# Perceiver megakernel on one core: three of thirteen subtractions of the maximum on GpSimd, full turns of the last context rows, scan rows fetched singly

## The chip, the cores and the metric

The kernel runs as one program on one core of a Trainium2 chip. The core has TensorE (PE; its weight loads are listed apart as PEld), VectorE (DVE), ScalarE (ACT), GpSimd (POOL) and SyncE (SP), which here only issues DMAs. The metric is the device time of one execution in microseconds (us); the median of three runs is shown, and a few tenths of a per cent is what two runs differ by.

## The reference

Two layers work on a latent array x of 16 batches x 64 rows x 128 columns, with a context of 16 x 1601 x 128. Each layer is cross-attention, then a state-space block, then a feed-forward block, each added to x. Cut to what matters here:

```python
# cross-attention, 16 heads of 64, softmax over 1601 context rows and 64 latents
logits = einsum('bhld,bhsd->bhls', q * scale, k * scale)   # layer 1 masks some rows
w = softmax(logits, axis=-1)
out = einsum('bhls,bhsd->bhld', w, v).reshape(B, L, INNER) @ Wo
# state-space block of layer 0, a scan over 64 positions for each of 16 states
h = dA * h + dB * z_t[:, :, None]
y_t = einsum('bds,bs->bd', h, C_t)
```

## The kernel before

**Groups and steps.** The attention is worked in 64 groups: 2 layers x 16 batches x 2 halves of the heads. A group has 512 queries (8 heads x 64 latents) and 13 tiles of 128 context rows, twelve of the context (G = 12) and one of 64 context rows (REM) and the 64 latents; the one context row that is left over is handled apart (`apart`, `apart_weight`). The projections of keys and values are folded into the queries and the output weights, so a tile's scores are one matmul of the turned context `kvT` against the queries. One step n of the main loop in `run` (L1584) is one tile: `scores` (L693) multiplies into a PSUM bank `s` (three such banks), DVE takes the running maximum `R` over the tiles (L714 in layer 1, with the mask; L716 in layer 0), and ACT copies the scores to SBUF as `st` (L719 or L721). 23 steps (LAG) later `average` (L810) multiplies the weights with the context rows `kv` into `av`.

**The maximum.** When a group's 13 tiles are scored, `plan` (L1533) runs it through stages, counted in steps after its end. Step 0, `partial`: a reduction of R on DVE over blocks (L750) and `four` (L751). Step 2, `joint`: a transpose on PE (L758) and a reduction on DVE, `top` (L760). Step 3, `handed`: two DMAs, one on ACT's queue back into R (L765), one on SP into DRAM, `md` (L766). Step 5, `everywhere`: DVE spreads R's rows into `mb`, one of the three PSUM banks of the pool `tp` (L772). Step 7, `own_max`: SP reads md back as a column (L779). Step 11: the weight of the row apart (L786, L787). The last group has a plan of its own (`maximum`, `spread_max`).

**The weights.** From step 6 on, every second step, `weigh` (L802) takes two tiles: DVE subtracts mb from them in place (L807), ACT takes the exponential (L808). The seven calls have 2, 2, 2, 2, 2, 2 and 1 tiles, at steps 6 to 18; the last two are tiles 10 and 11, and tile 12. mb is released after the last of them. `gather` (L822) then forms the averages `aq` on DVE, `denominator` (L865) divides them on POOL (L869), `turn` (L871) transposes them and `output` (L886) multiplies with the output weights.

**Context.** `context` (L628) normalises a batch's context in layer 0, writes it to DRAM (`xh`), turns it on PE in four calls of up to four blocks (L685; the last call is one block of 64 rows), and ACT scales each call twice, into `kvT` and into `kts`, which goes to DRAM for layer 1. The rows 64 to 127 of the last block are set to zero beforehand (L518, L656). `with_latents` (L612) multiplies kv by the norm's weights on POOL (L624).

**Scan.** `scan0` (L899) works on 256 of 1024 rows at a time. For each of 16 states s, `ahead` (L969) makes the decays `da` on ACT (L977) and the inputs `db` on POOL (L978); then come DVE's scan (L989), DVE's product with the row of C (L994) and POOL's sum (L995). The rows of B and C for a state are broadcast from DRAM to all partitions as `bb` (L974), for two states at a time, in two DMAs, with two buffers.

**What sets the order.** The text of the program gives each instruction its priority; a scheduler at build time then fixes each engine's order, an instruction going as soon as its inputs are expected to be there. `behind` (L1662) keeps side work behind the last score work on PE, ACT and DVE. On the chip every engine and every DMA queue works in that fixed order. Side work (context, queries, scan, experts, feed-forward) is drawn in between by budgets in `run`.

**cT.** In `scan1` (L1223) a tile `cT` holds the rows of C for layer 1's block (L1326); `th` (L1252) is the tile of a tanh that is read last at L1282.

Of the kernel before, what the change touches and what calls it, by code (L numbers as in the profile page):

```python
# [32 lines left out]
F32 = mybir.dt.float32  # L33
# [4 lines left out]
ALU = mybir.AluOpType  # L38
# [4 lines left out]
P = 128  # L43
NB, L, D = 16, 64, 128
# [3 lines left out]
G = 12  # L48
REM = 64
# [4 lines left out]
NQ = 512  # L54
# [2 lines left out]
PAIRS = 13  # L57
BLK = 32
LOWEST = -3.0e38

(LN1W, LN1B, LN2W, LN2B, NORMW, NORMB, G1, G2, YG1, YB1, YG2, YB2) = range(12)
LNOFF = 12
# [5 lines left out]
NS = 16  # L68
# [10 lines left out]
TG = CG * P  # L79
# [4 lines left out]
class Kernel:  # L84
# [543 lines left out]
    def context(self, lay, b):  # L628

        nc = self.nc  # L630
        w1, b1 = self.vecs_of(lay)[:2]
        kv, kvT = self.kv_of[lay, b]
        n = G + 1
        if (lay, b) == (0, 1):

            mv = self.sm([P, n, 2], "fmv", bufs=2)
            rstd, off = (self.sm([P, n], f"c{x}") for x in ("rstd", "off"))
            for k in range(n):
                bs = self.sm([P, 6], "fbs")
                nc.vector.bn_stats(bs, kv[:, k, :D])  # L640
                nc.vector.bn_aggr(mv[:, k, :], bs)
                if k % 2:
                    yield 1.0
            nc.vector.tensor_scalar_add(rstd, mv[:, :, 1], EPS)
            self.rsqrt(rstd, rstd, n)
            nc.gpsimd.tensor_tensor(off, mv[:, :, 0], rstd, ALU.mult)
            nc.gpsimd.tensor_scalar(off, off, -1.0, None, ALU.mult)
            for k in range(8, n):
                nc.gpsimd.tensor_scalar(kv[:, k, :D], kv[:, k, :D], mv[:, k, 0:1], rstd[:, k:k + 1], ALU.subtract, ALU.mult)
            yield HOP3  # L650
            for k in range(8):
                nc.scalar.activation(kv[:, k, :D], kv[:, k, :D], AF.Identity, scale=rstd[:, k:k + 1], bias=off[:, k:k + 1])
                if k % 2:
                    yield 1.0
        elif lay == 0:
            nc.gpsimd.memset(kv[64:P, G, :D], 0.0)  # L656
            nmean, rstd, v, off = (self.sm([P, n], f"c{x}") for x in ("mean", "rstd", "var", "off"))
            for lo, hi in ((0, 7), (7, n)):
                nc.vector.tensor_reduce(nmean[:, lo:hi], kv[:, lo:hi, :D], AX.X, ALU.add)
                if lo == 0:  # L660
                    yield 1.0
            nc.vector.tensor_scalar_mul(nmean, nmean, -1.0 / D)
            yield 0.2
            for k in range(n):
                scr = self.at.tile([P, D], F32, tag="cscr", name=f"scr{b}_{k}", bufs=1)
                nc.scalar.activation(scr, kv[:, k, :D], AF.Square, bias=nmean[:, k:k + 1], accum_out=v[:, k:k + 1])  # L666
                if k in (3, 6, 9):
                    yield 0.0
            yield HOP1
            nc.vector.tensor_scalar(v, v, 1.0 / D, 1e-5, ALU.mult, ALU.add)  # L670
            self.rsqrt(rstd, v, n)
            nc.gpsimd.tensor_tensor(off, nmean, rstd, ALU.mult)  # L672
            yield HOP5
            for k in range(n):
                nc.scalar.activation(kv[:, k, :D], kv[:, k, :D], AF.Identity, scale=rstd[:, k:k + 1], bias=off[:, k:k + 1])  # L675
                if k in (3, 6, 9):
                    yield 0.0
        if lay == 0:
            nc.sync.dma_start(out=self.xh[b], in_=kv[:, :, :D])
            yield HOP  # L680
            for g in range(G // 4 + 1):
                w, m = (512, P) if g < G // 4 else (REM, REM)
                t = self.tp(f"kt{b}_{g}")
                for k in range(4 * g, min(4 * g + 4, n)):
                    nc.tensor.transpose(t[:, (k - 4 * g) * P:(k - 4 * g) * P + m], kv[:m, k, :D], self.ident[:m, :m])  # L685
                raw = self.at.tile([P, 512], F32, tag="kts", name=f"kts{b}_{g}", bufs=1)
                for to, by in ((kvT[:, g * 512:g * 512 + w], w1), (raw[:, :w], YG1)):
                    nc.scalar.activation(to, t[:, :w], AF.Copy, scale=self.vcol[:, by:by + 1])
                nc.sync.dma_start(out=self.xhT[b][:, g * 512:g * 512 + w], in_=raw[:, :w])
                yield HOP3  # L690
        yield from self.with_latents(lay, b)
# [76 lines left out]
    def everywhere(self, g):  # L768
# [2 lines left out]
        grp["mb"] = self.tp(f"mb{g}")  # L771
        self.nc.vector.stream_shuffle(grp["mb"], grp["R"], [0] * BLK)  # L772

    def own_max(self, g):

        nc, grp = self.nc, self.groups[g]
        m4 = grp["m4"] = self.sm([P, 4], "m4")
        with nc.allow_non_contiguous_dma(reason="one number for each query"):
            nc.sync.dma_start(out=m4, in_=self.mdram[g].rearrange("(k f) j -> (f j) k", k=4))  # L779
# [22 lines left out]
    def weigh(self, g, j):  # L802

        nc, grp = self.nc, self.groups[g]
        st, mb = grp["st"][j], grp["mb"]
        n = min(2, NT - 2 * j)
        nc.vector.tensor_tensor(st, st, self.row(mb, [P, n, NQ]), ALU.subtract)  # L807
        nc.scalar.activation(st, st, AF.Exp)  # L808

    def average(self, g, i, j):  # L810
# [88 lines left out]
    def scan0(self, gr):  # L899
        nc, tc, a = self.nc, self.tc, self.a  # L900
        X = self.X[:, gr * CG:(gr + 1) * CG, :]
        with tc.tile_pool(name="sc1", bufs=1) as one, ExitStack() as later:
            t1 = lambda shape, name: one.tile(shape, F32, tag=name, name=f"sc_{name}")
# [21 lines left out]
            both = [P, 2, TG]  # L925
# [7 lines left out]
            g = self.tp("g")  # L933
            for k in range(2):
                nc.tensor.matmul(g[:, k * TG:(k + 1) * TG], W_gate[:, k * P:(k + 1) * P], xT, start=True, stop=True)
            th = t1(both, "y")
# [11 lines left out]
            t = self.tp("bc")  # L948
# [3 lines left out]
            bcd = self.dram.tile([2, NS, TG], F32, tag=f"bcd{gr}", name=f"bcd{gr}")  # L952
# [13 lines left out]
            y = t1(both, "y")  # L966
            yield 1.2

            def ahead(s):  # L969
                nonlocal bb  # L970
                if s % 2 == 0:
                    bb = work.tile([P, 2, 2, TG], F32, tag="bb", name=f"bb{s}")
                    for j in range(2):
                        nc.sync.dma_start(out=bb[:, j], in_=bcd[j, s:s + 2, :].partition_broadcast(P))  # L974
                da, db = (work.tile(both, F32, tag=n, name=f"{n}{s}") for n in ("da", "db"))
                for k in range(2):
                    nc.scalar.activation(da[:, k, :], dt[:, k, :], AF.Exp, scale=na[:, k, s:s + 1])  # L977
                nc.gpsimd.tensor_tensor(db, u, self.row(bb[:, 0, s % 2, :], both), ALU.mult)  # L978
                return da, db, self.row(bb[:, 1, s % 2, :], both)

            bb = None
            made = ahead(0)
            yield HOP
            for s in range(NS):
# [238 lines left out]
    def scan1(self, c0, CG):  # L1223
# [5 lines left out]
        with tc.tile_pool(name="sd1", bufs=1) as one, tc.tile_pool(name="sd2", bufs=CG) as work:  # L1229
# [93 lines left out]
                        nc.tensor.matmul(t[:, hh * TG:(hh + 1) * TG], m[:, k, hh * P:(hh + 1) * P], xc[:, k, :], start=(k == 0), stop=(k == 1))  # L1323
                nc.scalar.copy(dst.rearrange("p h t -> p (h t)"), t[:, :2 * TG])

            bT, cT = t1([P, 2, TG], "bT"), t1([P, 2, TG], "cT")  # L1326
            bc(bT, BwT)
            yield 0.4
            yield HOP1
# [198 lines left out]
    def run(self, out):  # L1528
# [2 lines left out]
        self.groups = [{"key": (lay, b, half)} for lay in range(2) for b in range(NB) for half in range(2)]  # L1531
        ng = len(self.groups)
        self.plan = (  # L1533
            ((0, self.partial), (2, self.joint), (3, self.handed), (5, self.everywhere), (7, self.own_max), (11, self.apart_weight)),
            ((1, self.maximum), (3, self.spread_max)),
        )
        per_layer = NB * 2 * NT
# [251 lines left out]
```

## Time and profile before

| | us |
|---|---|
| median of three runs | 1936.54 (1932.92 to 1939.88) |
| the profiled execution | 1938.11 |
| its span, first to last instruction | 1936.4 |
| PE busy | 1883.0 |
| PEld busy | 1426.3 |
| DVE busy | 1633.4 |
| ACT busy | 1357.9 |
| POOL busy | 511.8 |
| the subtractions L807 on DVE, 448 | 461.3 (two tiles each) + 42.9 (one tile) |
| the exponentials L808 on ACT, two tiles each, 384 | 404.1 |
| mean granted TensorE clock | 0.996 of full |

All lines of the profile name a line of the kernel, an engine, an operation and the tile that is written, an arrow, and the tiles that are read, with buffer numbers left out. "busy" is the time in which the engine works on at least one instruction of the group; "idle before" is the time in which it stood still ahead of them, and what ended that. In the list of waits, "ACT st L719 <- DVE R L714" says that ACT stood still ahead of its instruction on st at L719 until DVE's instruction on R at L714 had ended. "issue" is time with no wait that the profile shows.

### The profile page before, as it was taken

Reading aid. Unit: us, or ns where it says so; the run is one execution under the profiler, and the core shown is the slowest. Engines: PE = TensorE matmul, PEld = TensorE weight load, DVE = VectorE, ACT = ScalarE, POOL = GpSimd, SP = SyncE. Lnnn points to the kernel's source line nnn. Section 1 sums busy time; section 2 is a strip of 40 time slices with the busy share of each in tenths; the row PEclk is TensorE's granted clock in tenths of the full one; section 3 lists DMA queues with packets and bytes.
Section 4 is the critical chain, followed back from the end, with each engine's and each line's share of the span. In section 5 each row is a group of like instructions: output and inputs, shape, how many; then the busy total and the mean of one; then the engine's idle time right before and its main releaser. Section 6 shows DMA issues by size and latency. Waiting matters only on the chain. (4 is left out here: it accounts for less than half of the span.)

```text
span 1936.4 us, 32717 instructions
## 1 busy us (share of the span) xinstructions
PE 1883.0 (97%) x11738; PEld 1426.3 (74%) x11738; DVE 1633.4 (84%) x3186; ACT 1357.9 (70%) x2635; POOL 511.8 (26%) x584
## 2 busy tenths in 40 slices
PE   9999999998999999999999999999999999999998
PEld 5777777676777767777667787767778777776786
DVE  7987777998878998886998978999787998877984
ACT  5888887897869888776665757767566565765651
POOL 5122122543214453121443203453101121102000
PEclk9999999999999999999999999999999999999999
DMA  6121112321123131232232102222120211201100
GB/s 194 36 58 55 55 55 77 86 64 45 54 82 94 57 82 49 69 95 68 73 79 59 40 25 75 71 71 55 42 58 21 60 38 38 59 2 38 25 2 23
DMA packets 192268, 112.64 MB, mean 58 GB/s; under 512 B 56030, under 2 KB 174570, under 8 KB 192106
## 3 DMA queue, kind: packets, MB, share of 16 engines
q1 hardware_dynamic: 187278, 109.77, 20.6%
q8 instruction: 93, 1.52, 0.3%
q10 hardware_dynamic: 4828, 0.78, 0.2%
q14 instruction: 69, 0.57, 0.1%
HBM read 81.41 MB, written 27.54 MB: 56 GB/s over the span
## 5 line engine op out<-in xcount | busy, mean ns | idle before, releaser
L820 PEld LDWEIGHTS av<-kv,st 128*128 128x128 f32 x6656 | 870.2, 192 | 365.6 <-issue 346.3
L820 PE MATMUL av<-kv,st 128*128 128x129 f32 x6656 | 884.6, 276 | 2.2 <-DVE aq L829 2.1
L706 PE MATMUL s<-qT,kvT 128*128 128x512 f32 x1664 | 862.8, 601 | 15.7 <-ACT st L721 10.5
L808 ACT ACTIVATE st<-st 128x1024 f32<-128x1024 f32 (+1 forms) x448 | 444.4, 997 | 130.2 <-DVE st L807 124.2
L807 DVE TENSOR_TENSOR st<-st,mb 128x1024 f32<-128x1024 f32 (+1 forms) x448 | 504.2, 1130 | 2.0 <-PE mb L794 1.5
L719 ACT ACTIVATE st<-s,mcol 128x512 f32<-128x512 f32 x416 | 282.7, 683 | 219.4 <-DVE R L714 197.5
L721 ACT COPY st<-s 128x512 f32<-128x512 f32 x416 | 239.9, 582 | 108.1 <-DVE R L716 100.2
L714 DVE SCALAR_TENSOR_TENSOR R<-s,mcol,R 128x512 f32<-128x512 f32 x352 | 261.5, 743 | 57.2 <-PE s L706 55.2
L716 DVE TENSOR_TENSOR R<-s,R 128x512 f32<-128x512 f32 x352 | 240.2, 682 | 67.0 <-PE s L706 65.2
L706 PEld LDWEIGHTS s<-qT,kvT 128*128 128x128 f32 x1664 | 254.8, 192 | 35.9 <-ACT st L721 18.4
L624 POOL TENSOR_TENSOR kv<-kv,vec 128x384 f32<-128x384 f32 (+1 forms) x128 | 133.7, 1059 | 242.6 <-PE kt L685 68.9
L869 POOL TENSOR_TENSOR aq<-aq,rd 128x512 f32<-128x512 f32 x63 | 71.7, 1138 | 254.4 <-DVE rd L868 241.7
L978 POOL TENSOR_TENSOR db<-sc_u,bb 128x512 f32<-128x512 f32 x64 | 84.9, 1329 | 120.1 <-DVE h L989 61.2
L995 POOL TENSOR_TENSOR sc_y<-sc_y,h 128x512 f32<-128x512 f32 x60 | 79.6, 1327 | 117.6 <-DVE h L994 116.9
L989 DVE TENSOR_TENSOR_SCAN h<-da,db 128x512 f32<-128x512 f32 x64 | 85.7, 1339 | 0.0
L675 ACT ACTIVATE kv<-kv,coff,crstd 128x128 f32<-128x128 f32 x182 | 77.9, 494 | 8.5 <-POOL coff L672 8.5
L829 DVE SCALAR_TENSOR_TENSOR aq<-xeb,ee,av 128x129 f32<-128x129 f32 x252 | 76.7, 339 | 0.6 <-issue 0.4
L666 ACT ACTIVATE scr<-kv,cmean 128x128 f32<-128x128 f32 x182 | 72.3, 397 | 0.8
L498 PE MATMUL q<-xnT,wqk 128*128 128x128 f32 x512 | 68.4, 277 | 2.7 <-ACT qT L507 2.3
L498 PEld LDWEIGHTS q<-xnT,wqk 128*128 128x128 f32 x512 | 63.0, 192 | 7.7 <-ACT qT L507 2.5
L139 POOL TENSOR_TENSOR crstd<-cvar,neghalf 128x13 f32<-128x13 f32 x14 | 34.8, 2487 | 120.5 <-DVE cvar L670 98.9
L892 PEld LDWEIGHTS o<-wvo,aT 128*128 128x128 f32 x512 | 59.4, 192 | 5.3 <-issue 3.6
(425 smaller groups left out, 1821.4 us busy)
## 6 DMA issues: line engine op xcount, KB each, us to landing
bb<-bcd SPq DMA_DIRECT2D x64, 256.0 KB
xh<-kv SPq DMA_DIRECT2D x16, 832.0 KB
kv<-xh SPq DMA_DIRECT2D x16, 832.0 KB
kvT<-xhT SPq DMA_DIRECT2D x16, 800.0 KB
kv<-in_ctx_dram SPq DMA_DIRECT2D x15, 768.0 KB
xhT<-kts SPq DMA_DIRECT2D x45, 256.0 KB
ew<-in_e1T_dram SPq DMA_DIRECT2D x36, 64.0 KB
ew<-in_e3T_dram SPq DMA_DIRECT2D x36, 64.0 KB
```

Source lines behind the costliest of these rows:

```text
L498: nc.tensor.matmul(t[:, k * P:(k + 1) * P], self.wqk[:, g * 4 + k, :], xnT, start=True, stop=True)
L624: nc.gpsimd.tensor_tensor(kv[:, lo:hi, :D], kv[:, lo:hi, :D], self.row(self.vec[:, w1, :], [P, hi - lo, D]), ALU.mult)
L706: mm = nc.tensor.matmul(s, self.kv_of[lay, b][1][:, i * P:(i + 1) * P], q, start=True, stop=True)
L714: mx = nc.vector.scalar_tensor_tensor(R, s, mc, last, ALU.add, ALU.max)
L716: mx = nc.vector.tensor_tensor(R, s, last, ALU.max)
L719: ev = nc.scalar.activation(st, s, AF.Identity, bias=mc)
L721: ev = nc.scalar.copy(st, s)
L807: nc.vector.tensor_tensor(st, st, self.row(mb, [P, n, NQ]), ALU.subtract)
L808: nc.scalar.activation(st, st, AF.Exp)
L820: nc.tensor.matmul(grp["av", j][:, k, :], st, self.kv_of[lay, b][0][:, i, :], start=(i == 0 and k == 0), stop=(i == NT - 1 and k == 1))
L978: nc.gpsimd.tensor_tensor(db, u, self.row(bb[:, 0, s % 2, :], both), ALU.mult)
L989: nc.vector.tensor_tensor_scan(flat(h), flat(da), flat(db), 0.0, ALU.mult, ALU.add)
```

## The change

For all groups but the last, weigh steps 5 and 6 no longer subtract on DVE. A new stage at step 6 broadcasts md from DRAM to all partitions (`wide`, one buffer of 128 x 512 in SBUF), and three new stages at steps 10, 12 and 14 subtract wide from tiles 10, 11 and 12 on POOL, in place. In `context` the last block is turned with all 128 rows; only its first 64 columns are used, as before. In `scan0` the rows of one state come in one DMA, for the current and the next state, in three buffers of half the size. In `scan1` cT takes the buffer of th. Each of these two gives back 2 KB of every partition in its own stage; wide takes 2 KB in all of them.

```diff
+SIDE = (10, 11, 12)
...
             for g in range(G // 4 + 1):
-                w, m = (512, P) if g < G // 4 else (REM, REM)
+                w = 512 if g < G // 4 else REM
                 t = self.tp(f"kt{b}_{g}")
                 for k in range(4 * g, min(4 * g + 4, n)):
-                    nc.tensor.transpose(t[:, (k - 4 * g) * P:(k - 4 * g) * P + m], kv[:m, k, :D], self.ident[:m, :m])
+                    nc.tensor.transpose(t[:, (k - 4 * g) * P:(k - 4 * g + 1) * P], kv[:, k, :D], self.ident)
...
+    def broadcast(self, g):
+        wide = self.groups[g]["wide"] = self.at.tile([P, NQ], F32, tag="wide", name=f"wide{g}", bufs=1)
+        self.nc.sync.dma_start(out=wide, in_=self.mdram[g].rearrange("c j -> (c j)").partition_broadcast(P))
+    def lowered(self, g, i):
+        grp = self.groups[g]
+        st = grp["st"][i // 2][:, i % 2, :]
+        self.nc.gpsimd.tensor_tensor(st, st, grp["wide"], ALU.subtract)
...
-        nc.vector.tensor_tensor(st, st, self.row(mb, [P, n, NQ]), ALU.subtract)
+        if g == len(self.groups) - 1 or 2 * j not in SIDE:
+            nc.vector.tensor_tensor(st, st, self.row(mb, [P, n, NQ]), ALU.subtract)
         nc.scalar.activation(st, st, AF.Exp)
...
+            def fetch(s):
+                x = fetched[s] = work.tile([P, 2, TG], F32, tag="bb", name=f"bb{s}", bufs=3)
+                nc.sync.dma_start(out=x, in_=bcd[:, s, :].partition_broadcast(P))
             def ahead(s):
-                nonlocal bb
-                if s % 2 == 0:
-                    bb = work.tile([P, 2, 2, TG], F32, tag="bb", name=f"bb{s}")
-                    for j in range(2):
-                        nc.sync.dma_start(out=bb[:, j], in_=bcd[j, s:s + 2, :].partition_broadcast(P))
+                for x in range(s, min(s + 2, NS)):
+                    if x not in fetched and x not in done:
+                        fetch(x)
+                bb = fetched.pop(s)
+                done.add(s)
...
-                nc.gpsimd.tensor_tensor(db, u, self.row(bb[:, 0, s % 2, :], both), ALU.mult)
-                return da, db, self.row(bb[:, 1, s % 2, :], both)
+                nc.gpsimd.tensor_tensor(db, u, self.row(bb[:, 0], both), ALU.mult)
+                return da, db, self.row(bb[:, 1], both)
...
-            bT, cT = t1([P, 2, TG], "bT"), t1([P, 2, TG], "cT")
+            bT, cT = t1([P, 2, TG], "bT"), one.tile([P, 2, TG], F32, tag="th", name="sd_cT")
...
-            ((0, self.partial), (2, self.joint), (3, self.handed), (5, self.everywhere), (7, self.own_max), (11, self.apart_weight)),
+            ((0, self.partial), (2, self.joint), (3, self.handed), (5, self.everywhere), (6, self.broadcast), (7, self.own_max), (11, self.apart_weight),
+             *((10 + 2 * k, lambda p, i=i: self.lowered(p, i)) for k, i in enumerate(SIDE))),
```

More of the change, by code (lines that the diff above doesn't have):

```diff
@@ L977, in ahead @@
                     nc.scalar.activation(da[:, k, :], dt[:, k, :], AF.Exp, scale=na[:, k, s:s + 1])
-                nc.gpsimd.tensor_tensor(db, u, self.row(bb[:, 0, s % 2, :], both), ALU.mult)
-                return da, db, self.row(bb[:, 1, s % 2, :], both)
-            bb = None
+                nc.gpsimd.tensor_tensor(db, u, self.row(bb[:, 0], both), ALU.mult)
+                return da, db, self.row(bb[:, 1], both)
+            fetched, done = {}, set()
             made = ahead(0)
```

## The prediction

> **What bounds the kernel now.** I read the page's first part, then the busy times by stretch, then the waits of PE, ACT and DVE, and last the groups by shape.
>
> ```profile
> PE 1883.0 (97%) x11738; PEld 1426.3 (74%) x11738; DVE 1633.4 (84%) x3186; ACT 1357.9 (70%) x2635; POOL 511.8 (26%) x584
> ```
>
> PE is the bound: 53.4 us of 1936.4 idle. No change off PE can give more than that, and much of it lies where this change doesn't act. Busy times by stretch (us of PE, PEld, DVE, ACT, POOL; instructions in brackets):
>
> ```profile
> 100.00:1800.00 1700.00, 1660.71 (x10280) 1256.44 (x10279) 1452.10 (x2733) 1226.50 (x2371) 466.97 (x503) 1.00 0.21 58
> ...
> 300.00:400.00 100.00, 95.58 (x548) 69.24 (x547) 88.42 (x144) 82.45 (x175) 44.33 (x40) 1.00 0.31 85
> ...
> 500.00:600.00 100.00, 100.00 (x605) 77.87 (x605) 81.33 (x186) 76.92 (x181) 20.79 (x28) 1.00 0.19 52
> ...
> 700.00:800.00 100.00, 93.84 (x603) 69.95 (x602) 84.23 (x141) 82.18 (x187) 31.93 (x31) 1.00 0.22 61
> ...
> 1400.00:1500.00 100.00, 100.00 (x680) 78.97 (x679) 80.21 (x169) 59.96 (x100) 11.72 (x17) 0.99 0.15 40
> ```
>
> Between 100 and 1800 us PE idles 1700 - 1660.7 = 39.3 us; the other 14 are the start and the tail, which the change leaves alone. Sort the 17 stretches of 100 us by DVE's share: in the eight with DVE at 83.5 us or less PE idles 7.1 us in all (0.9 each), in the nine above it 32.2 (3.6 each). So PE starves where DVE is full. The waits say how (total us, times, longest):
>
> ```profile
> ACT st L719 <- DVE R L714: 197.5, 202, 5.5
> ACT st L808 <- DVE st L807: 124.2, 186, 3.3
> ACT st L721 <- DVE R L716: 100.2, 104, 4.3
> ...
> PE s L706 <- ACT st L721: 10.5, 15, 1.7
> PE s L706 <- ACT st L719: 4.6, 8, 1.1
> PE tm L758 <- DVE four L751: 3.6, 6, 1.3
> ```
>
> The running maximum R, in DVE's queue behind the subtractions, holds ACT's copy of the scores; that copy frees the PSUM bank, and the next score matmul waits for it. Of PE's idle time 24.1 us is named after DVE's or ACT's lateness in this loop: 15.1 (scores), 3.6 (tm), 2.2 (WvT for X, L896), 2.1 (av for aq, L829), 1.1 (mq for L807).
>
> **The subtractions leave DVE.** Groups by shape (busy, mean ns, idle before):
>
> ```profile
> L807 DVE TENSOR_TENSOR st<-st,mb 128x1024 f32<-128x1024 f32 x384 | 461.3, 1207 | 2.0 <-PE mb L794 1.5
> ...
> L989 DVE TENSOR_TENSOR_SCAN h<-da,db 128x512 f32<-128x512 f32 x64 | 85.7, 1339 | 0.0
> ...
> L994 DVE TENSOR_TENSOR h<-h,bb 128x512 f32<-128x512 f32 x60 | 48.0, 799 | 0.0
> ...
> L807 DVE TENSOR_TENSOR st<-st,mb 128x512 f32<-128x512 f32 x64 | 42.9, 671 | 0.0
> ```
>
> There are 2 layers x 16 batches x 2 halves = 64 groups; all but the last lose weigh step 5 (tiles 10 and 11) and step 6 (tile 12): 63 x (1207 + 671 ns) = 118.3 us off DVE. They run back to back (idle before 2.0 us), so they are queue that R, top and aq stand behind, not path by themselves: what they are worth is what PE waits for that queue.
>
> **They arrive on POOL.** 63 x 3 = 189 subtractions of 128x512 with both inputs in SBUF. L978 and L995 are the same shape: median 1273 ns each (the means, 1329 and 1327, include collisions). 189 x 1.27 = 240 us; POOL goes from 512 to 752 us, 39%. POOL isn't on PE's path while it is on time. Is it? In the timeline of each of the 63 groups, counted from the end of top (L760): the m read (L779), which waits for the landing of md just as the new broadcast will, issues after 1.4 us (median; at most 7.0). A 256 KB bb transfer took 3.4 to 4.4 us from issue to the start of the waiting db. So wide is there after some 5.3 us (at most 11.4), and three subtractions end 3.8 us later: 9.1, at most 15.2. The exponential of tiles 10 and 11 starts now after 26.0 us (median), 18.2 (10th percentile), 12.3 (shortest). Wide's one buffer was last read a group earlier, 13 steps, so the broadcast doesn't wait for it. Behind a subtraction that waits for wide stand aq (L869, for the turn L880), the context's kv (L624) and the scan's db and sc_y; each of them would be late by some us and has as much slack as POOL's idle before it (254, 243, 120, 118 us in all). Median slack 17 us; only a handful of groups are tight, and those have ACT running ahead of PE. I cost it at 2 us. ACT also loses the wait for L807 before two of seven exponentials, 2/7 of 124 = 35 us; DVE's part of it is the same time and not counted again.
>
> **Contention.** DVE instructions with two SBUF inputs grow when POOL works beside them: L989 has median 1215 and longest 2222 ns, L994 680 and 1590, L751 226 and 1289, and means above the medians by 8.0, 7.1 and 13.2 us in all. That is 28 us at 512 us of POOL work; 240 us more gives 28 x 240/512 = 13 us, at most twice that. L807 itself (mb in PSUM) never shows it: 1222 ns is its longest. DVE's net gain is 118 - 13 = 105 us, at worst 92: in the body 1452 falls to 1347 of 1700, 79%, which is below where stretches idle.
>
> The Trainium skill, "SBUF — State Buffer", section "Who interferes with whom", says that a VectorE instruction with two SBUF inputs and a GpSimd instruction that reads SBUF exclude each other for the whole instruction. This speaks against the change. The rows agree in size (2222 - 1215 is nearly one POOL operation); if each of the 189 blocked DVE once for its whole length, the move would cost DVE as much as it frees. The rows give 28 us for all POOL work of today, so I stay with them.
>
> **DMA.** 63 broadcasts of 256 KB on SP (an issue of this kind, L974, takes 0.42 us there) are 27 us of SP and 16 MB beside 112.6. The wait for md on SP (L779, 62.6 us today) only moves in front of the broadcast. The row m comes at most one issue later; its reader L786 runs 19.5 us (median) after top. Nothing.
>
> **Scan rows.** The count (64 issues of 256 KB) stays; rows come one step earlier. What goes is POOL's wait db <- bb, 33.2 us in 14 times. The scan L989, which follows db, has idle 0.0 before it: hidden, 0. Should the earlier issue stand longer on SP for its buffer (L974 waits 144 us today), md and wide behind it would be late by some us, inside the slack above.
>
> **Last context rows.** A turn of 64 rows (L685, 15 of them) starts 205 ns after the matmul before it and the next starts 202 ns after it; between full ones these steps are 112 and 109. 15 x 186 ns = 2.8 us of PE gained; doubling its columns costs nothing that the 109 doesn't hold. "TensorEngine Tiling (Array Packing)", "Key Properties", of the Trainium skill says that a change of tiling mode drains TensorE, which would explain the 0.2 us on either side.
>
> **cT in th's buffer.** Its last reader before (L1282) is long done: 0. **mb leaves its PSUM bank at step 14 instead of 18**, so the three tp buffers have one more for 4 of 13 steps. No row isolates this; the nearest waits are PE at <- ACT mo_xT (3.0) and mv <- ACT mo_q (1.3): 0 to 4.3, I take 1.
>
> **Sum.** What DVE's relief gives PE: the nine full stretches falling to the level of the others would give 9 x (3.6 - 0.9) = 24; half of the 24.1 us of named waits would give 12. I take the middle, 18. With turns 2.8, bank 1, lateness of POOL -2: 20 us. The profiled execution took 1938.11 us (span 1936.4 and 1.7 around it); 1918 follows. It lies 1.6 us above the median of the three runs, 1936.54, so the prediction is 1917.
>
> **Rivals.**
> - *DVE was full but not the cause.* The idle stretches are also those of the scan and the experts, with waits such as me <- sg (2.9) or syt <- sd_y (3.2) that are latencies of small chains; the stretch at 1200 has DVE at 95.6 and idles only 1.8. Then only the turns and the bank remain: 1936.5 - 4 = 1933 (1926 to 1941).
> - *All of it goes.* Shorter queues on DVE remove the whole 39 us of the body and the turns add 2.8: 1936.5 - 42 = 1895 (1890 to 1908).
> - *Slower: POOL is late.* POOL works in order, and today waits up to 27.4 us for rd (L869), 30.0 for av (L621), 20.8 for cvar (L139). Subtractions queued behind such a wait by more than the 17 us of slack hold the exponential on ACT, behind it the copies of scores, and so PE. If half of the groups are late by one POOL operation, that is 31 x 1.27 = 39 us against the 20 gained: 1956. For it: these waits are long. Against it: they are mostly POOL waiting with nothing else to do, and the subtractions are ready 10 us before.
>
> **Chances.** Forecast (1908 to 1926) 0.58; not the cause 0.18; all of it 0.13; POOL late 0.11. About 0.3% (1930.7 to 1942.3) is what a measurement can tell from no change. Faster: 0.58 + 0.13 + a third of 0.18 = 0.77; same 0.12; slower 0.11. The range drops the slower case and the far edge of the fast one: 1894 to 1942.
>
> **What would show it.** Right: DVE near 1530 us, POOL near 755, L807 on 63 x 5 + 7 = 322 instructions; PE idle between 100 and 1800 near 20 us; "PE s <- ACT st" under 8; L685 all 128x128; POOL hardly named before L808. Wrong: a wait of ACT's exponential for POOL above 20 us; the means of L989, L994 and L751 up by more than 30%; PE idle unchanged with DVE down.

## The result, and the profile after

The changed kernel takes 2027.62 us (median of 4 runs, 2026.29 to 2030.78) where the kernel before takes 1935.3 beside it: ratio 1.0482, interval 1.0466 to 1.0498. It is slower by some 92 us; the prediction was 1917, with a range of 1894 to 1942. The profiled execution has a span of 2025.0 us against 1936.4. One execution of one kernel below (work cut to four elements) ran at a lower granted clock, 0.946, and took 1958 us where its other three took 1922 to 1923; it is left out of that kernel's time.

The first part of the page of the changed kernel:

```profile
span 2025.0 us, 32875 instructions
...
PE 1912.2 (94%) x11738; PEld 1442.8 (71%) x11738; DVE 1562.5 (77%) x3060; ACT 1345.6 (66%) x2635; POOL 763.4 (38%) x773
```

The work moved as intended: DVE is 71 us less busy, POOL 252 us more. PE's idle time went from 53.4 to 112.8 us (+59.4), and PE's busy time, for the same 11738 matmuls, rose by 29.2. Together these are the 88.6 us. So two things are to be explained: who starves PE, and why its matmuls got longer. The body of the kernel (us of PE, PEld, DVE, ACT, POOL; then granted clock):

```profile
100.00:1800.00 1700.00, 1608.15 (x9762) 1212.15 (x9761) 1320.21 (x2475) 1170.11 (x2297) 679.07 (x655) 0.98 0.26 66
```

Idle there is 91.9 us in place of 39.3, although DVE is less busy than before. The list of waits (total us, times, longest):

```profile
POOL st L784 <- DMA wide<-md: 267.1, 41, 19.3
ACT st L720 <- DVE R L715: 195.4, 187, 5.5
ACT st L821 <- POOL st L784: 176.9, 68, 8.7
ACT st L722 <- DVE R L717: 109.1, 120, 5.2
ACT st L821 <- DVE st L820: 47.9, 72, 3.3
...
PE s L707 <- ACT st L720: 28.7, 19, 5.2
PE s L707 <- ACT st L722: 26.1, 23, 6.1
```

The first and the third line are new: POOL stands 267.1 us ahead of its subtractions for wide, and ACT stands 176.9 us ahead of exponentials (L821) for POOL's subtraction (L784). ACT's wait for DVE's subtraction fell from 124.2 to 47.9, more than the 35 us forecast, but what took its place is larger. PE's wait for the copies of scores rose from 15.1 to 54.8 us.

One such place, in the timeline of ACT (start, duration, instruction, idle before and its releaser):

```profile
979.05 0.89 ACT L994 ACTIVATE da<-sc_dt,na 128x256 f32<-128x256 f32 x2
986.53 1.06 ACT L821 ACTIVATE st<-st 128x1024 f32<-128x1024 f32 x1 [6.58 <-POOL st L784]
987.49 0.67 ACT L720 ACTIVATE st<-s,mcol 128x512 f32<-128x512 f32 x1
```

and of PE in the same microseconds:

```profile
981.96 1.05 PE L833 MATMUL av<-kv,st 128*128 128x129 f32 x8
988.22 2.07 PE L707 MATMUL s<-qT,kvT 128*128 128x512 f32 x2 [5.21 <-ACT st L720]
```

ACT stands 6.58 us for POOL; the copy of a score tile (L720) is the next instruction behind it, keeps its PSUM bank, and PE stands 5.21 us. In this group top had ended at 974.5. POOL began its first two subtractions at 983.57, when wide had landed, and ended them at 986.5, 12 us after top. The third ended at 989.0, 14.4 after top. That is no later than the prediction allowed (at most 15.2). What is new is that ACT was already there.

The order of ACT's instructions, read off the two built programs for group 10 (line, tile):

```
before                 changed
L808 st10_0            L821 st10_5   <- tiles 10 and 11
L808 st10_1            L821 st10_6   <- tile 12
L808 st10_2            L821 st10_0
L808 st10_3            L821 st10_1
L808 st10_4            L821 st10_2
L808 st10_5            L821 st10_3
L808 st10_6            L821 st10_4
```

Before, all 64 groups have the order 0 to 6. In the changed program 4 have it; in 51 the exponential of step 5 stands ahead of that of step 0, in 36 of these the order is 5, 6, 0, 1, 2, 3, 4. The program's build orders each engine's instructions by its own estimate of when their inputs are ready. Steps 5 and 6 no longer need mb or a place in DVE's queue, so they probably looked ready first (the estimates themselves are not on record). Of the 68 waits, ACT reached the exponential a median 6.2 us after top (3.1 to 13.6), where before that exponential began 26.0 after.

The longer matmuls: granted clock is the last but two of the columns here, in the stall behind 697 us and after it:

```profile
697.40:700.40 3.00, 0.25 (x3) 0.06 (x1) 3.00 (x4) 0.96 (x2) 3.00 (x2) 1.00 0.02 6
700.40:707.20 6.80, 5.24 (x14) 3.65 (x15) 3.80 (x12) 6.80 (x13) 4.89 (x7) 0.50 0.17 56
707.20:712.00 4.80, 4.80 (x31) 3.60 (x30) 4.35 (x9) 4.80 (x11) 1.43 (x2) 1.00 0.85 227
```

PE does next to nothing for 3 us (its stall lasts 4.3 us, to 701.9), and the clock is then 0.50 for the 6.8 us that follow. Apart from the end, the trace of the changed kernel has 16 such stretches of 3.4 or 6.8 us, that of before 4, all of 3.4 us. Half their length, those at the end included, is 37.0 us of full clock lost against 8.6: 28 us, about the 29.2 by which PE's busy time grew. (Counting only the time in which PE was busy in them, it is 32.6 against 6.8, or 26 us.) Such a stall is paid twice. Not every stall is: of the 32 above 1.0 us in the changed kernel 15 lead into half clock and 17 don't.

### The profile page after: what moved, and what is told of

The parts are those of the page before. It is cut to its first block, busy times and chain, and to the rows that moved or that the text cites. A ratio compares the mean times of both kernels' runs of the same rounds, so it can differ in the third digit from the quotient of the medians.

```text
span 2025.0 us, 32875 instructions
## 1 busy us (share of the span) xinstructions
PE 1912.2 (94%) x11738; PEld 1442.8 (71%) x11738; DVE 1562.5 (77%) x3060; ACT 1345.6 (66%) x2635; POOL 763.4 (38%) x773
## 5 line engine op out<-in xcount | busy, mean ns | idle before, releaser
L833 PEld LDWEIGHTS av<-kv,st 128*128 128x128 f32 x6656 | 879.9, 194 | 376.5 <-issue 356.1
L707 PE MATMUL s<-qT,kvT 128*128 128x512 f32 x1664 | 876.6, 610 | 55.8 <-ACT st L720 28.7
L821 ACT ACTIVATE st<-st 128x1024 f32<-128x1024 f32 (+1 forms) x448 | 441.0, 997 | 226.7 <-POOL st L784 176.9
L720 ACT ACTIVATE st<-s,mcol 128x512 f32<-128x512 f32 x416 | 281.2, 684 | 216.9 <-DVE R L715 195.4
L820 DVE TENSOR_TENSOR st<-st,mb 128x1024 f32<-128x1024 f32 x322 | 386.4, 1206 | 2.2 <-PE mb L806 1.5
L784 POOL TENSOR_TENSOR st<-st,wide 128x512 f32<-128x512 f32 x189 | 247.7, 1337 | 353.7 <-DMA wide<-md 267.1
L1012 POOL TENSOR_TENSOR sc_y<-sc_y,h 128x512 f32<-128x512 f32 x60 | 84.4, 1406 | 54.2 <-DVE h L1011 54.2
L1006 DVE TENSOR_TENSOR_SCAN h<-da,db 128x512 f32<-128x512 f32 x64 | 92.9, 1451 | 1.0 <-ACT da L994 1.0
```

Of the source, the lines that this page charges most:

```text
L707: mm = nc.tensor.matmul(s, self.kv_of[lay, b][1][:, i * P:(i + 1) * P], q, start=True, stop=True)
L720: ev = nc.scalar.activation(st, s, AF.Identity, bias=mc)
L784: self.nc.gpsimd.tensor_tensor(st, st, grp["wide"], ALU.subtract)
L833: nc.tensor.matmul(grp["av", j][:, k, :], st, self.kv_of[lay, b][0][:, i, :], start=(i == 0 and k == 0), stop=(i == NT - 1 and k == 1))
L1006: nc.vector.tensor_tensor_scan(flat(h), flat(da), flat(db), 0.0, ALU.mult, ALU.add)
```

## Experiments

All ratios are to the kernel before, run beside each kernel on the same chip (medians 1935.0 to 1936.1). A ratio need not be that of the two medians: in the first run below these would give 1.0068. "In order" means with the first edit below.

**The order of the exponentials alone.** Each exponential of a group is ordered behind the one before it (an ordering for the build, with no wait added):

```
-        nc.scalar.activation(st, st, AF.Exp)
+        x = nc.scalar.activation(st, st, AF.Exp)
+        if j:
+            self.later(x, grp["exp"])
+        grp["exp"] = x
```

> The changed kernel, with one edge for the build-time order: the exponential of each weigh call stands behind that of the call before it, so those of tiles 10 to 12 come last again on ACT. Theory A (the exponentials of tiles 10 to 12 were put ahead of the first one in ACT's order and hold ACT, and behind it the copies of scores, until POOL is done): 1905 to 1932 us, ACT's wait for POOL's subtraction falls from 176.9 us to under 20, PE clock back at 0.99 or more. Theory B (POOL's 189 operations slow DVE by their use of SBUF): 2000 to 2030, whatever the order. Theory C (wide lands too late): 1990 to 2030, the wait for POOL stays over 100 us.

Measured 1948.22 us, 1.0059 (1.0042 to 1.0076). 79 of the 92 us (82 by the ratios) come back by an edit of ACT's order. Theory A's signs came (no wait for POOL, clock 0.992), but its time, 1905 to 1932, did not. In the built programs the edit shifts others a little as well: some 60 of DVE's instructions and 20 of PE's stand elsewhere, which was not tried apart. ACT's wait for POOL has left the list, though POOL ends its three subtractions as late as before (median 9.9 us after top, 10.1 in the changed kernel):

```profile
PE s L707 <- ACT st L720: 9.5, 16, 1.5
PE s L707 <- ACT st L722: 9.4, 16, 1.5
PE tm L759 <- DVE four L752: 8.0, 10, 2.6
```

54.8 us became 18.9. But the kernel is still 0.6% slower than before, not faster.

**Everything but the subtractions.** No broadcast, no work on POOL, all subtractions on DVE:

```
-        if g == len(self.groups) - 1 or 2 * j not in SIDE:
-            nc.vector.tensor_tensor(st, st, ...)
+        nc.vector.tensor_tensor(st, st, ...)
-  (6, self.broadcast), ... *((10 + 2 * k, lowered ...) ...)
```

> Only the full turns, the scan rows fetched singly and cT in th's buffer; all subtractions on DVE as before. Theory A and B: 1926 to 1938 us, the turns' 2.8 us gained and nothing lost. Rival D (the earlier fetch holds SP, and md and others behind it): over 1950.

Measured 1935.26, 0.9991 (0.9977 to 1.0004): turns, scan rows and cT together are not to be told from nothing.

**The turns alone** (before, with the last context rows turned 128 at a time):

```
...
-  ...(t[:, (k - 4 * g) * P:(k - 4 * g) * P + m], kv[:m, k, :D], self.ident[:m, :m])
+  ...(t[:, (k - 4 * g) * P:(k - 4 * g + 1) * P], kv[:, k, :D], self.ident)
```

> The kernel before with full turns alone. 15 x 186 ns = 2.8 us less: 1930 to 1936; the step from the matmul before such a turn falls from 205 to 112 ns and the one after it from 202 to 109. If the drain between modes was not the cause of these steps, they stay.

Measured 1932.98, 0.9987 (0.9975 to 0.9999): some 2 us. In its trace the steps into and out of the 15 last turns are 112 and 109 ns (206 and 202 before). Why a turn of 64 rows costs the longer steps, the run doesn't show.

**The relief alone.** In order, no broadcast, POOL's work left out (and with it the subtraction for steps 5 and 6):

```
-  (6, self.broadcast), ... *((10 + 2 * k, lowered ...) ...)
```

> The changed kernel with the three subtractions and the broadcast left out in 63 groups, so that tiles 10 to 12 go to the exponential without the maximum taken off, in the order of calls: what DVE's relief of 118 us alone is worth, with nothing on POOL. The prediction's step (18 us from the relief, 3 from the turns) gives 1915; if DVE was not the cause of PE's idle time, 1930 to 1934; if all of PE's idle time in the body goes, 1895.

Measured 1919.24, 0.9909 (0.9888 to 0.9929): 0.0082 under the kernel with everything but the subtractions, so the relief of DVE, with the earlier release of mb's bank, is worth 16 us. The forecast's gain existed. Its page and body:

```profile
PE 1875.8 (98%) x11738; PEld 1424.5 (74%) x11738; DVE 1538.8 (80%) x3060; ACT 1354.4 (71%) x2635; POOL 515.7 (27%) x584
```

```profile
100.00:1800.00 1700.00, 1670.73 (x10382) 1267.79 (x10381) 1379.15 (x2639) 1235.43 (x2388) 471.90 (x505) 0.99 0.23 59
```

PE idles 29.3 us there, 10.0 less than before. Against the kernel in order, POOL's part of the change costs 29 us. The next runs ask why.

**Is the order bad by itself?** As the last, without the edit that keeps the order: 60 of 64 groups then have 5, 6, 0, 1, 2, 3, 4, but these tiles wait for nobody.

> The changed kernel without the broadcast, without GpSimd's subtractions and without anything that holds the exponentials in order: in 60 of 64 groups those of steps 5 and 6 then stand ahead of step 0, as in the changed kernel, but what they read is there early. Left out: the maximum is not subtracted from the tiles of steps 5 and 6. Theory (the order costs only because GpSimd's result comes late): 1917 to 1925, as the 1919 us in order. Rival (the order itself costs, since the exponentials of steps 0 to 4 come later): 1945 or more.

Measured 1915.76, 0.9895 (0.9879 to 0.9912). The order costs nothing where the inputs are there. What costs is an instruction placed early whose input comes late. (POOL has no added work in this kernel; the early order with that work, but with nobody waiting for it, was not run.)

**POOL's work with nobody waiting for it.** In order; the three operations run on wide itself:

```
-        self.nc.gpsimd.tensor_tensor(st, st, grp["wide"], ALU.subtract)
+        self.nc.gpsimd.tensor_tensor(grp["wide"], grp["wide"], grp["wide"], ALU.subtract)
```

> The changed kernel with the exponentials kept in order, in which GpSimd's three operations of a group have the broadcast copy itself as both operands and as result, so that they cost GpSimd the same and nobody waits for them; left out: the maximum is not subtracted from the tiles of steps 5 and 6. Without the broadcast and the three operations this kernel takes 1919 us, with them and their wait 1948. Theory (the 29 us are GpSimd's work itself, beside VectorE's and ahead of the scan's own GpSimd work): 1940 to 1950, VectorE's busy time near 1568 us. Rival (the 29 us are ScalarE's wait for the three results): 1917 to 1926, VectorE's busy time near 1540 us. About 1933 would share it.

Measured 1942.38, 1.0033 (1.0020 to 1.0046). Of the 29 us only about 5 go with the result being needed, and the two intervals overlap.

**The transfer alone.** In order, with the broadcast, without POOL's operations.

> The changed kernel with the exponentials kept in order and the broadcast copy fetched, but without GpSimd's three operations; left out: the maximum is not subtracted from the tiles of steps 5 and 6. Theory (the transfer costs nothing by itself): 1917 to 1922, as the 1919 us without it. Rival (the transfer takes SyncE's queue or the DMA engines from the scan's rows and the carried rows): 1930 or more, with more waits of the scan for its rows.

Measured 1922.79, 0.9933 (0.9916 to 0.9950): 5 us above the relief alone, with intervals that overlap, and 1 us above the theory's range. At most a small part.

**One tile in place of three** (`SIDE = (12,)`, at step 14):

> The changed kernel with the exponentials kept in order and only the last tile (12) subtracted on GpSimd; the full pairs all on VectorE. VectorE is relieved of 63 x 671 ns = 42 us in place of 118, GpSimd gets 63 x 1.3 = 82 us in place of 247. Theory (relief and GpSimd's cost both go with the number of operations): the 16 us of relief become 6, the 29 us of cost become 10, so 1935 + 4 = 1937 to 1941. Rival (the cost is a wait that only the first of the three or the broadcast sets): the whole 29 us stay or go, 1929 or 1958.

Measured 1942.87, 1.0036 (1.0023 to 1.0049), in neither range. If a third of the relief is worth 5 us, the cost is 14: half of the 29, not a third. One operation in place of three doesn't turn the sign.

**Only the first 28 groups** (of 64; the others subtract on DVE):

> The changed kernel with the exponentials kept in order and GpSimd's three subtractions only in the first 28 of the 64 groups, all others on VectorE. Theory (the relief is worth its 13 us in the groups ahead of step 364, the cost there is 7 us, and what comes later is the kernel before): 1935.3 - 6 = 1927 to 1932. Rival (what is gained early is given back later, since later stages are bound by something else): 1934 to 1938.

Measured 1933.40, 0.9984 (0.9974 to 0.9994), between the two. In its trace the score matmuls of step 364 (of 832, two matmuls each) come 8.1 us earlier than before, step 468 5.5 and the end 6.4 (one execution of each; by the medians the gain is 2.7): most of what the early groups gain seems to be kept, it is only less than hoped. This kernel and the one with the turns alone are the fastest that compute the reference, 0.2% and 0.1% under the kernel before, less than the 0.3% that the prediction sets for telling a change from none.

**Work on a resting tile, first try.** In order, no broadcast; POOL's three operations on a tile that nobody reads, whole and on one partition:

```
+        self.still = self.at.tile([P, NQ], F32, tag="wide", name="still", bufs=1)   # once
-        self.nc.gpsimd.tensor_tensor(st, st, grp["wide"], ALU.subtract)
+        self.nc.gpsimd.tensor_tensor(x, x, x, ALU.subtract)     # x = still, or still[:1]
```

> The changed kernel with the exponentials in order, without the broadcast, and with GpSimd's three operations of a group on a tile that lies in SBUF from the start and that nobody reads: GpSimd does the same work but never stands at its head for a transfer. Left out: the maximum is not subtracted from the tiles of steps 5 and 6. The same operations behind the transfer took 1942 us, the transfer alone 1923. Theory (GpSimd's work beside VectorE's is what costs): 1936 to 1943. Rival (GpSimd standing up to 19 us for the transfer, with the scan's and the context rows' work behind it, is what costs): 1919 to 1926.

> The changed kernel with the exponentials in order, without the broadcast, and with GpSimd's three operations of a group on one partition of a tile that lies in SBUF from the start: neither the wait for the transfer nor 128 partitions. Left out: the maximum is not subtracted from the tiles of steps 5 and 6. Theory (time on GpSimd beside VectorE is what costs): as with 128 partitions of the same tile, 1936 to 1943. Rival (the wait or the partitions): as with none of the operations, 1917 to 1924.

Measured 2051.89 (1.0598, 1.0582 to 1.0614) and 2050.42 (1.0591, 1.0575 to 1.0607): neither theory. The page of the first, in 40 slices of the span (tenths busy):

```profile
PE   6825479999999999999999999999999999999998
...
POOL 7999941135421235421244320345211111111010
```

Operations that depend on nothing were all put at the front of POOL's queue, some 200 us in one piece, and PE starved meanwhile (its wait at <- aq on POOL alone is 32.3 us). After that the kernel runs as with the relief alone: it is 131 us behind the kernel before at score step 104 and 116 at the end, a gain of 15. These two say nothing on the question they were made for, but show the same force as the main result: what a dependency held in place moves when the dependency goes.

**One partition.** As with nobody waiting, on one partition of wide in place of 128 (`grp["wide"][:1]`):

> The changed kernel with the exponentials in order, with the broadcast, and with GpSimd's three operations on one partition of the broadcast copy in place of 128: the wait for the transfer stays, the work touches one partition. Left out: the maximum is not subtracted from the tiles of steps 5 and 6. Theory (what costs is the work beside VectorE's, which goes by time and not by partitions): 1938 to 1943 if one partition takes GpSimd as long as 128, and VectorE's busy time near 1556 us. Rival (it goes by the partitions touched): 1922 to 1930, VectorE near 1541 us.

Measured 1945.88, 1.0049 (1.0033 to 1.0066). An operation takes 1.09 us on one partition and costs PE as much as 128 do.

**Work without the wait, wait without the work.** The first has the operations on the resting tile, each ordered for the build behind its group's shuffle, and no broadcast; the second has broadcast and operations at their places, cut to four elements:

```
+        op = self.nc.gpsimd.tensor_tensor(x, x, x, ALU.subtract)    # x = still
+        self.later(op, grp["shuffled"])
```
```
+        x = grp["wide"][:1, :4]
+        self.nc.gpsimd.tensor_tensor(x, x, x, ALU.subtract)
```

> The changed kernel with the exponentials in order, without the broadcast, and with GpSimd's three operations of a group on a resting tile that nobody reads, each held by the build's order behind the shuffle of its group's maximum: the same 189 operations at about the same places of GpSimd's queue, without the wait for the transfer. Left out: the maximum is not subtracted from the tiles of steps 5 and 6. Theory (the work beside VectorE's costs the 20 us): 1934 to 1941, VectorE's busy time near 1556 us. Rival (the wait at the queue's head costs them): 1917 to 1925, VectorE near 1540 us.

> The changed kernel with the exponentials in order, with the broadcast, and with GpSimd's three operations of a group cut down to four elements of one partition of the broadcast copy: the wait for the transfer at the same places of GpSimd's queue, next to no work. Left out: the maximum is not subtracted from the tiles of steps 5 and 6. Theory (the work beside VectorE's costs the 20 us): 1921 to 1927, as the transfer alone. Rival (the wait at the queue's head costs them): 1936 to 1944. About 1932 for both kernels would share it.

Measured 1936.81, 1.0004 (0.9991 to 1.0016), and 1921.84, 0.9935 (0.9918 to 0.9951). The wait costs no more than the transfer alone; the work costs 0.0095, 18 us, over the relief alone. What of the work?

**As long on POOL, without reads; and with one read.** As the work without the wait, with two memsets for each operation, or with a constant added:

```
-        op = self.nc.gpsimd.tensor_tensor(x, x, x, ALU.subtract)
+        op = self.nc.gpsimd.memset(x, 0.0)                             # twice
+        op = self.nc.gpsimd.tensor_scalar(x, x, 0.0, None, ALU.add)    # the other kernel
```

> As the kernel with GpSimd's work at its place on a resting tile, but each of the 189 operations is two memsets of that tile in place of one subtraction: GpSimd's time at the same places of its queue, with nothing read from SBUF. Left out: the maximum is not subtracted from the tiles of steps 5 and 6. Theory (reads of SBUF by GpSimd shut out VectorE's instructions with two inputs there): 1917 to 1925, and VectorE's busy time back from 1571 us to near 1540, if the memsets take GpSimd 100 us or more in all. Rival (GpSimd's own later work coming late): 1930 to 1941, with VectorE's time as it may be.

> As the kernel with GpSimd's work at its place on a resting tile, but each of the 189 operations adds a constant to the tile, so that one input is read from SBUF in place of two. Left out: the maximum is not subtracted from the tiles of steps 5 and 6. Theory (any read of SBUF by GpSimd shuts VectorE out for the length of the instruction): 1930 to 1941 if it takes GpSimd about as long as the subtraction, VectorE's busy time 1555 us or more. Rival (only two inputs do): 1917 to 1925, VectorE near 1540.

Measured 1921.75, 0.9932 (0.9915 to 0.9948), as its theory has it, and 1929.09, 0.9961 (0.9948 to 0.9974), between theory and rival. In the traces of these two and of the kernel with the subtractions, PE, DVE, ACT and the rest of POOL do the same instructions in the same order, so a changed order is no rival here. The first lines are the memsets, then the subtractions of the resting tile, then the additions (min/median/max ns):

```profile
L788 POOL MEMSET still<- x378: 515/525/569, 47.8 to 1822.1; 128x512 f32 x189
```
```profile
L787 POOL TENSOR_TENSOR still<-still x189: 1029/1040/1992, 47.9 to 1838.0; 128x512 f32<-128x512 f32 x189
```
```profile
L787 POOL TENSOR_SCALAR still<-still x189: 1480/1491/2429, 47.6 to 1833.2; 128x512 f32<-128x512 f32 x189
```

2 x 525 ns is as long as 1040, at the same places, and the cost is 0.0023 in place of 0.0095. So most of the cost (0.0072 of 0.0095) is POOL's reading and not its time; with one input read it costs 0.0052, for 1.4 times as long. Why about half, no run shows. The longest memset is 569 ns; the longest of the two that read has grown by nearly 1 us. DVE shows the other side, pages of the kernel with memsets and with subtractions:

```profile
PE 1875.2 (98%) x11738; PEld 1423.6 (74%) x11738; DVE 1546.0 (81%) x3060; ACT 1355.1 (71%) x2635; POOL 709.5 (37%) x963
```
```profile
PE 1881.8 (97%) x11738; PEld 1426.4 (74%) x11738; DVE 1571.0 (81%) x3060; ACT 1354.8 (70%) x2635; POOL 721.0 (37%) x774
```

DVE does the same 3060 instructions in 1546.0 and 1571.0 us; the sums of their durations are 1728.4 and 1751.1, 22.7 us apart. The two groups that grew most, four (4.8 us) and the scan (3.3), are among the three that the prediction named. Here are both with the subtractions, and PE's wait of tm for four:

```profile
L1013 DVE TENSOR_TENSOR_SCAN h<-da,db 128x512 f32<-128x512 f32 x64 | 91.8, 1435 | 0.0
...
L752 DVE TENSOR_TENSOR four<-part,sx 128x64 f32<-128x64 f32 x63 | 32.4, 515 | 0.9
...
PE tm L759 <- DVE four L752: 8.2, 11, 2.0
```

with memsets the means are 1383 and 439 ns and the wait for four 5.9 us. The third group of the prediction, the product with C's row, did not grow (854 against 867 ns). But 8.8 of the 22.7 us lie in tensor_scalar instructions, which read one tile and some numbers for each partition: the norm into xn has 483 ns against 362. So it isn't only DVE's work with two inputs that grows.

Instruction by instruction: take those of DVE that last 100 ns or more above the median of their group with the relief alone. In each of these traces every one of them overlaps an instruction of POOL in time. Put down to the instruction of the longest overlap, the excess beside the 189 operations is 27.7 us with subtractions, 12.0 with additions and 4.1 with memsets; beside POOL's other work it is 54 to 55 us in all three.

The Trainium skill, "SBUF — State Buffer", section "Who interferes with whom", says that VectorE with two SBUF inputs contends with a GpSimd instruction that reads SBUF, not with one that only writes it. The pair of 1.0004 and 0.9932 agrees, and so do the 27.7 and 4.1 us; the instructions with one tile to read, which grew too, that sentence doesn't cover.

## Why the prediction was wrong

The sum of the runs, in parts of the time before, each the difference of two neighbouring kernels: turns, scan rows and cT -0.0009; DVE's relief -0.0082 (-16 us); the transfer +0.0024 and POOL's work behind it +0.0100 (together 24 us); the results needed, in order, +0.0026 (5 us); the exponentials out of order +0.0423 (82 us). That makes 1.0482, as a chain of differences must; parts of 5 us and less are no larger than what the intervals leave open.

**The step that failed: "They arrive on POOL", costed at 2 us.** Its times for POOL were about right: the third subtraction ends a median 10.1 us after top, at most 17.5 (forecast 9.1, 15.2). It compared them with when "the exponential of tiles 10 and 11 starts now", 26.0 us after top, and called the difference slack. But that time was held by mb, by DVE's queue and by the order 0 to 6, and the change removed the first two, from which the build had made the third. In the changed kernel ACT reached the exponentials it had to wait for a median 6.2 us after top. The slack of 17 us belonged to the kernel before. That the order is the cause is shown from both sides: late results in order cost 5 us more than results nobody needs; the order without late results costs nothing; both together 82 us more.

**The halved clock** had no term. In the changed kernel it makes 26 to 28 of the 89 us.

**Contention, 13 us, at most 26, was sized low, and its price was wrong.** In the changed kernel DVE's durations sum to 21.5 us more than with the relief alone (1737.3 against 1715.8), inside the bound. The 13 came from three groups, 28 us in the kernel before. Counted over all of DVE's groups, the instructions 100 ns or more above their median make 47.7 us there, and all 86 overlap work of POOL; 47.7 x 240/512 = 22 would have been the size. With the operations on the resting tile it is 35 us (1751.1).

The step took these microseconds off DVE's relief, at the relief's rate of 18 us of PE for 105 us of DVE. The relief earned 16 for 118, as costed. The added ones cost PE more: 18 us for 35 on the resting tile, and 19 for 16 (1734.9 against 1718.7) where the operations stand behind the transfer, against the transfer alone. So the price isn't a sixth, but it isn't one number either. That the lengthened instructions are those PE waits for next (four, the norms ahead of an expert) is read from the waits, not tested by itself; in the changed kernel four's mean even fell, from 436 to 393 ns. That reading is the cause is shown on the resting tile alone. Behind the transfer POOL's own results also come later: DVE's waits for POOL, mostly norms waiting for rstd, are 45.0 us in all against 37.5 with the transfer alone (35.7 on the resting tile). The two weren't separated there. In the whole, POOL's work outweighs the relief even with the order mended.

**The relief's 18 us were met by 16, in part by luck.** PE's idle time in the body fell by only 10.0 us; the rest is PE's busy time, 7.2 us lower in the trace with the relief than before, of which the prediction had only the turns' 2.8. And "PE starves where DVE is full" holds only coarsely: in the prediction's nine full stretches PE idles 5.2 us each in the five with DVE at 84 to 89 us, but 1.6 each in the four above 91.

**"DVE near 1530"** came out at 1562.5; with the relief alone it is 1538.8. The sum of DVE's durations fell by the 118 us forecast (1833.6 to 1715.8), but neighbouring instructions overlap in the records, so busy time fell by 95.

**What held.** The turns: 2.0 us for 2.8, each step as forecast. Scan rows and cT: nothing to be seen. The transfer: near nothing; from wide's issue to the start of the subtraction waiting for it were 3.2 to 5.9 us (41 times, median 3.6), near the 3.4 to 4.4 read off the bb rows. The bank of mb was not tried by itself; what it gives is inside the 16 us.

**The rivals.** "Slower: POOL is late" had the right sign and engine and the wrong mechanism: POOL's subtractions didn't stand behind rd, av or cvar by more than the slack, and the price of 39 us is less than half. Of the signs listed, "a wait of ACT's exponential for POOL above 20 us" was the one that spoke (176.9). "Means up by more than 30%" didn't: L989's is up 8%, L994's 7%, L751's is down. "DVE was full but not the cause" is refuted by the relief alone.

## What to carry to other kernels

The slack of an operand is read against the consumer's place after the change, not before: where a change takes away what an instruction waited for, look at what else that wait had kept in order, and if the order is made by a program, fix it and test it alone. Time freed on a queue that is nearly full is worth a fraction of itself, and time added in front of what the bounding engine waits for next may cost most of it, so the two aren't netted at one rate. Moving an elementwise operation to GpSimd frees VectorE only as far as its reads don't lengthen VectorE's own work beside them.

## What the runs showed of the hardware

- The granted clock fell to 0.5 behind some PE stalls of 1.3 us and more: for 3.4 us behind stalls of 1.3 to 3.0 us, for 6.8 us behind those of 3.3 to 6.1 (15 of the 16 stretches of the changed kernel; the first lies behind 0.9 us). Stalls of up to 2.85 us there, and one of 3.04 us in the kernel before, did not lead to it. The Trainium skill, "TensorE: Matmul & The Clock Gate", section "What's actually happening", gives the half clock after at least one idle window of about 3.4 us; here stalls shorter than that were enough.
- Where a stall falls in time is part of it. The changes of the clock lie on a grid of 3.41 us: between the starts at 447.79, 700.38 and 853.98 us there are 74 and 45 steps. If the trace of the changed kernel is cut along this grid, each of the 13 pieces at full clock with PE busy for less than 44% was followed by half clock, and none with more than 62%; in between, 4 were and others weren't. (In the kernel before, one piece with 42% was not.)
- GpSimd's 128x512 subtraction took a median 1.04 us with one tile as both inputs and 1.28 us with two tiles; on one partition 1.09 us (mean; 1.11 on 128), and cost PE no less than on 128 (1.0049 against 1.0033).
- Adding a constant, with one input to read, took longer (1.49 us) than subtracting two, and cost PE about half as much (0.0052 against 0.0095).
